# Nine-tap scans with 13 products a line in place of 14, and sums of weights moved to VectorE

## The chip, the cores and the metric

The kernel runs on one core of a Trainium2 chip. The metric is the device time of one execution in microseconds (us); less is better. The engines of the core are TensorE (PE in the profile; PEld is its loading of weights), VectorE (DVE), ScalarE (ACT), GpSimd (POOL) and SyncE (SP), which here only issues transfers. They work at the same time and wait for each other by semaphores. SBUF is the memory on the chip; PSUM holds what TensorE writes.

## The reference

Four layers, each added to its own input after a group normalisation over a float32 image of 2 x 128 channels x 128 x 128: axial attention along one axis, four directional scans, a deformable 3x3 convolution, and a 4x4 convolution with stride 2 in a Hadamard basis. The change is in the second layer, the scans:

```python
def _pass_once(x, w, vertical, reverse):      # w: 128 x 128 x 9
    ...                                       # flipped or transposed for its direction
    def step(carry, xi):
        y = xi + relu(_conv1d(carry, w))      # nine taps along the line, padded by 4
        return (y, y)
    _, ys = lax.scan(step, xs[0], xs[1:])
...
x = _pass_once(x, w_ud, vertical=True, reverse=False)
x = _pass_once(x, w_du, vertical=True, reverse=True)
x = _pass_once(x, w_lr, vertical=False, reverse=False)
x = _pass_once(x, w_rl, vertical=False, reverse=True)
```

Each line of 128 pixels needs the finished line before it, so a scan is 127 dependent steps, and the four scans follow each other.

## The kernel before

Channels lie on the 128 partitions. Both images are held in one tile `both` (views `res[n]`) and are worked on together: a line is 2 images x 128 pixels, split into even and odd pixels of 2 x 64 each. `program` calls, in turn, the attention (`layer0_attention`), `Merge.run` (which also gives the sum of the input and the attention), `layer1` (the scans), `layer2` and `layer3`.

A scan step in `layer1` (line 1103) works from three SBUF tiles of the line before, `lines[turn]`: even pixels e, odd pixels o, and their sum, each with a margin of four. The nine taps are split into four pairs and one single tap, so that the two outputs of a pair of pixels share work: 14 products for 18. TensorE makes three PSUM groups in this order: `pl0` from e (five products with the even taps), `pl1` from o (four products with the odd taps, 65 columns wide, because the even output reads it at one place and the odd output one place further), `pl2` from the sum (the first tap, and four sums of neighbouring taps that are prepared in `ws`). A product is a float32 matmul of 128x128 weights on 2 x 64 or 2 x 65 columns; the profile records it as two matmuls. Then

- ScalarE copies `pl0` to `c0`;
- VectorE adds `pl1` and `c0` to `v`, and a relu-add (`scalar_tensor_tensor`: larger of v and 0, plus the line's own input) writes the new even pixels;
- VectorE adds the shifted `pl1` and `c0` to `u`, subtracts it from `pl2`, and a second relu-add writes the new odd pixels;
- VectorE adds even and odd pixels to the new sum.

In scans 0 to 2 (numbered from 0) ScalarE copies the new pixels back into the image; in scan 3 GpSimd writes them with the layer's input added. In scan 0 ScalarE also normalises each line, four lines ahead (`normalise`). Scans 0 and 1 go over rows, scans 2 and 3 over columns, so that there the image is read and written in strides. PSUM and temporaries have two and three buffers.

The order on TensorE, VectorE, ScalarE and GpSimd within the scans is the order written: they are wrapped in `InOrder` (line 75), which is why nearly everything stands under line 83. Around that, a planner places instructions by when it expects them to be ready: so the first sum of taps, written after the attention, stands on GpSimd's queue among the attention's last instructions, and transfers on SP's queue may pass each other.

`scan_weights` (line 1093) loads a scan's nine taps on ScalarE's queue and has GpSimd add pairs of them to `ws`, in one instruction of 128x512. `prepare()` in `layer1` runs `layer3_weights` (line 1808): it loads the last layer's weights (`ta`) on SP's queue, combines them on GpSimd in 25 operations of 128x256, which fall into the first lines of scan 0, and stores them (`w3_d`). SP's queue also writes the layer's input to `x1_d` and re-sorts it into column blocks, eight copies to `x1c_d` (line 1138), which scan 3 reads.

Of the kernel before, what the change touches and what calls it, by code (L numbers as in the profile page):

```python
# [1091 lines left out]

def scan_weights(env, prm, pool, d):

    nc = env.nc
    wl = pool.tile([P, 9, P], F32, name=f"wl{d}", tag=f"wl{d}")
    nc.scalar.dma_start(out=wl, in_=prm["wscan"][:, d])
    ws = pool.tile([P, 4, P], F32, name=f"ws{d}", tag=f"ws{d}")
    nc.gpsimd.tensor_tensor(ws, wl[:, 2:9:2, :], wl[:, 1:8:2, :], ALU.add)
    return wl, ws  # L1100


def layer1(env, prm, res, both, x1_d, x1c_d, st_gn, st_next, first, prepare):

# [4 lines left out]
    nc, tc = env.nc, env.tc  # L1109
    HS = S // 2  # L1110
    with ExitStack() as ctx:
# [1 line left out]
            for n in range(N):  # L1113
                nc.sync.dma_start(out=x1_d[:, n, lo:hi, :], in_=res[n][:, lo:hi, :])
        cp = ctx.enter_context(tc.tile_pool(name="l1c", bufs=1))
        sp = ctx.enter_context(tc.tile_pool(name="l1s", bufs=3))
        with tc.tile_pool(name="l1pn", bufs=1, space=PSUM) as pn:
            gs, gb = env.group_norm(cp, pn, st_gn, "l1")
        pp = ctx.enter_context(tc.tile_pool(name="l1ps", bufs=2, space=PSUM))
        weights = [first] + [scan_weights(env, prm, cp, d) for d in range(1, 4)]  # L1120
        prepare()
        xp = ctx.enter_context(tc.tile_pool(name="l1x", bufs=2))


        lines = [
            [cp.tile([P, N, HS + 4], F32, name=f"ln{k}{j}", tag=f"ln{k}{j}") for k in range(3)]
            for j in range(2)
        ]
        for pair in lines:
            for t in pair:  # L1130
                nc.vector.memset(t, 0.0)
        pe, dve, act, pool = (
            InOrder(tc, e) for e in (nc.tensor, nc.vector, nc.scalar, nc.gpsimd)
        )
# [16 lines left out]
        def normalise(h):  # L1151
            for n in range(N):
                act.activation(
                    res[n][:, h, :],
                    res[n][:, h, :],
                    AF.Identity,
                    bias=gb[:, n : n + 1],
                    scale=gs[:, n : n + 1],
                )


        ahead = 4
        for h in range(ahead):
            normalise(h)
        turn = 0
        for d in range(4):
            steps = list(range(S)) if d % 2 == 0 else list(range(S - 1, -1, -1))
            wl, ws = weights[d]
            if d == 3:
                columns = {w0: load_columns(w0) for w0 in (S - CB, S - 2 * CB)}  # L1170
            for at, line in enumerate(steps):
                here = [
                    both[:, :, line, k::2] if d < 2 else both[:, :, k::2, line] for k in range(2)
                ]
                if d == 0 and line + ahead < S:
                    normalise(line + ahead)
                last, now = lines[turn], lines[1 - turn]
                turn = 1 - turn
                new = [t[:, :, 2 : 2 + HS] for t in now]
# [5 lines left out]
                if at == 0:  # L1185
                    for k in range(2):
                        dve.tensor_copy(new[k], here[k])
                    dve.tensor_tensor(new[2], new[0], new[1], ALU.add)
                    if d == 3:
                        for k in range(2):  # L1190
                            pool.tensor_tensor(here[k], new[k], add[k], ALU.add)
                    continue
                ps = [
                    pp.tile([P, N, HS + (k == 1)], F32, name=f"pl{k}", tag=f"pl{k}")
                    for k in range(3)
                ]
                for k in range(3):
                    taps = 4 if k == 1 else 5
                    for j in range(taps):
# [10 lines left out]
                            start=(j == 0),  # L1210
                            stop=(j == taps - 1),
                        )
                c0 = sp.tile([P, N, HS], F32, name="c0", tag="c0")
                u = sp.tile([P, N, HS], F32, name="u", tag="u")
                v = sp.tile([P, N, HS], F32, name="v", tag="v")
                act.copy(c0, ps[0])
                dve.tensor_tensor(v, ps[1][:, :, 0:HS], c0, ALU.add)
                dve.scalar_tensor_tensor(new[0], v, 0.0, here[0], ALU.max, ALU.add)
                dve.tensor_tensor(u, ps[1][:, :, 1 : HS + 1], c0, ALU.add)
                v = sp.tile([P, N, HS], F32, name="v", tag="v")  # L1220
                dve.tensor_tensor(v, ps[2], u, ALU.subtract)
                dve.scalar_tensor_tensor(new[1], v, 0.0, here[1], ALU.max, ALU.add)
                dve.tensor_tensor(new[2], new[0], new[1], ALU.add)
                if d == 0:

                    for k in range(2):
                        for n in range(N):
                            act.copy(res[n][:, line, k::2], new[k][:, n])
                    continue
                if d < 3:  # L1230
                    for k in range(2):
                        act.copy(here[k], new[k])
                    continue
                for k in range(2):
                    pool.tensor_tensor(here[k], new[k], add[k], ALU.add)
                if line % RT >= 2 and line < S - RT:
# [559 lines left out]
def layer3_views(t):  # L1796


    a, b = 8 * P, 8 * P + 4 * P
    ws = t[:, 0:a].rearrange("p (k y o) -> p k y o", y=2, o=P)  # L1800
    wt = [
        part.rearrange("p (k r y o) -> p k r y o", r=2, y=2, o=P // 2)
        for part in (t[:, a:b], t[:, b : b + 8 * P])
    ]
    return ws, wt


def layer3_weights(env, prm, w3_d):

    nc, tc = env.nc, env.tc  # L1810
    H = P // 2
    one, two = slice(0, H), slice(H, P)
    add, sub = ALU.add, ALU.subtract
    with tc.tile_pool(name="l3w", bufs=1) as wp:
        ta = wp.tile([P, 4, 4, P], F32, name="ta", tag="ta")
        tb = wp.tile([P, 4, 4, P], F32, name="tb", tag="tb")
        tk = [wp.tile([P, 4, 2, H], F32, name=f"tk{k}", tag=f"tk{k}") for k in range(2)]
        w3 = wp.tile([P, W3], F32, name="w3w", tag="w3w")
        ws, wt = layer3_views(w3)
        nc.sync.dma_start(out=ta.rearrange("p u v o -> p (u v o)"), in_=prm["w3"])  # L1820
        pool = nc.gpsimd
        zero = wp.tile([P, 2 * P], F32, name="zero", tag="zero")
        pool.memset(zero, 0.0)

        def less(to, a, b):

            pool.tensor_tensor(to, a, b, add)
            none = zero.rearrange("p (k o) -> p k o", o=H)
            if len(to.shape) == 4:
                none = zero.rearrange("p (k y o) -> p k y o", y=2, o=H)  # L1830
            pool.tensor_tensor(to, none, to, sub)

        firsts = ((0, 3, add), (0, 3, sub), (2, 1, add), (2, 1, sub))
        seconds = ((3, 1, sub), (3, 1, add), (2, 0, sub), None)
        for part, plan in ((one, firsts), (two, seconds)):
            for k in range(4):
                to = tb[:, k, :, part]
                if plan[k] is None:
                    less(to, ta[:, :, 2, part], ta[:, :, 0, part])
                else:  # L1840
                    x, y, op = plan[k]
                    pool.tensor_tensor(to, ta[:, :, x, part], ta[:, :, y, part], op)
        for half, (part, plan) in enumerate(((one, firsts), (two, seconds))):
            for k in range(4):
                to = ws[:, :, k, part] if k < 2 else tk[half][:, :, k - 2, :]
                if plan[k] is None:
                    less(to, tb[:, :, 2, part], tb[:, :, 0, part])
                else:
                    x, y, op = plan[k]
                    pool.tensor_tensor(to, tb[:, :, x, part], tb[:, :, y, part], op)  # L1850
        for half in range(2):
            x, y = (tk[half][:, k : k + 2] for k in (0, 2))
            to = [wt[half][:, k] for k in range(2 + 2 * half)]
            pool.tensor_tensor(to[0], x, y, add)
            pool.tensor_tensor(to[1], x, y, sub)
            if half == 1:
                pool.tensor_tensor(to[2], y, x, sub)
                less(to[3], x, y)
        nc.sync.dma_start(out=w3_d, in_=w3)


def layer3(env, prm, res, w3_d, st_gn, out):
# [174 lines left out]
def program(ctx, tc, prm, out):  # L2037
# [33 lines left out]
    res = [both[:, n] for n in range(N)]  # L2071
    with tc.tile_pool(name="l1w", bufs=1) as wp:
        first = scan_weights(env, prm, wp, 0)
        merge.run(prm, res, mv, st_gn[1])
        merging.close()
        layer1(
            env,
            prm,
            res,
            both,  # L2080
            x1_d,
            x1c_d,
            st_gn[1],
            st_gn[0],
            first,
            lambda: layer3_weights(env, prm, w3_d),
        )
    layer2(env, prm, res, mem, tables, st_gn[0], st_gn[1])
    layer3(env, prm, res, w3_d, st_gn[1], out)
# [130 lines left out]
```

## Time and profile before

| what | us |
|---|---|
| median of 3 runs (5308.6 to 5312.2) | 5308.91 |
| profiled execution, its own time | 5305.85 |
| its span, first to last instruction | 5304.1 |
| scan 0, from its first sum of a line to that of scan 1 | 405.8 |
| scan 1, the same | 398.6 |
| scan 2, the same | 409.3 |
| scan 3, first to last sum | 417.1 |

TensorE is busy for 4974.9 us of the span, VectorE for 3521.7, ScalarE for 2658.8, GpSimd for 2126.1. The granted TensorE clock is 1.00 in the scans.

How to read it: a row of the timeline has the start in us, the duration in us, the engine, the line of the code, the operation, what it writes and from what, and how many instructions were merged; in brackets stands how long the engine had been idle and what ended that. A row of a tile's answer has the engine, operation, count, shortest/median/longest duration in ns, and the first and last start. `pl` stands for all three PSUM groups, `ln` for all of a line's tiles, `c` for `c0`. A busy TensorE is not TensorE at its peak, and idle time of an engine that nobody waits for costs nothing.

### The profile page before, as it was taken

How to read it: one execution, taken by the hardware profiler on the slowest of the kernel's cores; microseconds unless marked ns; L12 is line 12 of the kernel's file. 1: busy time of each engine (PE TensorE's matmuls, PEld its weight loads, DVE VectorE, ACT ScalarE, POOL GpSimd, SP SyncE). 2: the span in 40 equal slices, each digit the busy share in tenths (PEclk: the TensorE clock that was granted, in tenths of full speed). 3: DMA queues.
4: the chain of work that ended last, by engine and by line, in shares of the span. 5: the costliest groups of instructions: out<-in, count | busy, mean ns of one | idle time of the engine just before them, and what ended most of it. 6: DMA issues, size and time to landing. Idle time of an engine off the chain costs nothing. (4 is left out here: it accounts for less than half of the span.)

```text
span 5304.1 us, 179050 instructions
## 1 busy us (share of the span) xinstructions
PE 4974.9 (94%) x76283; PEld 4306.7 (81%) x76283; DVE 3521.7 (66%) x6818; ACT 2658.8 (50%) x7718; POOL 2126.1 (40%) x1749
## 2 busy tenths in 40 slices
PE   7898999999999934999999999999989999999999
PEld 6767888888888834999999999998468888888777
DVE  3636888888888857555555555666346666666688
ACT  3557898888889845554222332001334443443322
POOL 3214666666666634000000000333035555555576
PEclk8998999999999966999999999999989999999999
DMA  4362333333333369970000000101321111111011
GB/s 160 122 252 63 62 62 61 58 61 62 59 59 63 61 258 305 92 65 2 1 1 1 1 1 1 49 33 38 117 69 35 35 33 38 33 33 32 35 53 57
DMA packets 499988, 347.61 MB, mean 66 GB/s; under 512 B 311669, under 2 KB 456565, under 8 KB 487281
## 3 DMA queue, kind: packets, MB, share of 16 engines
q1 hardware_dynamic: 494144, 326.50, 27.0%
q8 instruction: 607, 9.95, 0.8%
q10 hardware_dynamic: 5040, 9.56, 0.5%
q14 instruction: 197, 1.61, 0.1%
HBM read 194.99 MB, written 157.72 MB: 66 GB/s over the span
## 5 line engine op out<-in xcount | busy, mean ns | idle before, releaser
L83 PE MATMUL pl<-ln,wl 128*128 128x128 f32 (+1 forms) x10160 | 1241.2, 276 | 9.3 <-DVE ln L83 7.8
L83 PEld LDWEIGHTS pl<-ln,wl 128*128 128x128 f32 x10160 | 1176.1, 190 | 22.3 <-issue 6.7
L83 POOL TENSOR_TENSOR w<-d 128x504 f32<-128x504 f32 x512 | 558.6, 1115 | 669.4 <-DVE s L83 612.8
L83 ACT ACTIVATE e<-e,mx 128x128 f32<-128x128 f32 x2048 | 793.4, 395 | 0.8 <-DVE mx L83 0.8
L83 POOL TENSOR_TENSOR res<-ln,x1t 128x128 f32<-128x128 f32 x256 | 149.3, 584 | 1428.2 <-DVE ln L83 1428.2
L83 POOL TENSOR_TENSOR e<-e,total 128x1024 f32<-128x1024 f32 x256 | 485.9, 1898 | 486.4 <-DVE total L83 477.1
L83 ACT COPY res<-ln 128x64 f32<-128x64 f32 (+1 forms) x1016 | 283.9, 304 | 702.2 <-DVE ln L83 702.2
L83 ACT COPY sm<-ps_s 128x1152 f32<-128x1152 f32 x256 | 286.6, 1119 | 562.6 <-PE ps_s L83 562.6
L83 PE MATMUL po<-sm,wdef 128*128 128x256 f32 x2304 | 567.5, 392 | 0.0
L83 PEld LDWEIGHTS ps_s<-s,xw 28*128 28x128 f32 x10240 | 456.6, 187 | 122.2 <-issue 77.2
L83 PE MATMUL pl<-ln,ws 128*128 128x128 f32 x4064 | 536.8, 273 | 0.0
L83 PE MATMUL ps_s<-s,xw 28*128 28x240 f32 (+2 forms) x10240 | 520.0, 343 | 16.4 <-DMA xw<-px_d 13.9
L83 POOL COPY et<-et 128x1024 f32<-128x1024 f32 x256 | 516.4, 2017 | 35.2 <-DVE et L83 27.0
L83 DVE TENSOR_TENSOR v<-pl,c 128x128 f32<-128x128 f32 x508 | 148.1, 291 | 540.7 <-PE pl L83 537.4
L83 PEld LDWEIGHTS pl<-ln,ws 128*128 128x128 f32 x4064 | 494.5, 190 | 0.0
L83 ACT ACTIVATE r<-gen,alphas 128x1536 f32<-128x1536 f32 x256 | 395.0, 1543 | 170.6 <-PE gen L83 143.6
L83 PEld LDWEIGHTS po<-sm,wdef 128*128 128x128 f32 x2304 | 418.4, 190 | 71.0 <-issue 0.2
L83 ACT ACTIVATION_READ_ACCUMULATOR e<-e,mx 128x1 f32 x2048 | 396.5, 194 | 0.0
L83 DVE SCALAR_TENSOR_TENSOR ln<-v,res 128x128 f32<-128x128 f32 x1016 | 347.0, 342 | 48.5 <-POOL res L83 0.9
L83 DVE STREAM_TRANSPOSE s<-w 128x1152 f32<-128x1152 f32 x256 | 349.8, 1367 | 33.0 <-PE ps_s L83 29.9
L83 PE MATMUL te<-cst_main,e 128*128 128x128 f32 x2048 | 338.5, 287 | 28.7 <-POOL e L83 20.9
L83 DVE COPY et<-te 128x512 f32<-128x512 f32 x512 | 348.2, 680 | 12.9 <-PE te L83 12.4
(246 smaller groups left out, 8405.5 us busy)
## 6 DMA issues: line engine op xcount, KB each, us to landing
xw<-px_d SPq DMA_DIRECT2D x528, 56.0 KB
xa<-in_x SPq DMA_DIRECT2D x16, 1024.0 KB
v_d<-vs SPq DMA_DIRECT2D x16, 1024.0 KB
qb_d<-sb SPq DMA_DIRECT2D x16, 1024.0 KB
qa_d<-sa SPq DMA_DIRECT2D x8, 2048.0 KB
zz<-qb_d SPq DMA_DIRECT2D x1024, 16.0 KB
vt<-v_d SPq DMA_DIRECT2D x64, 256.0 KB
qk<-qa_d SPq DMA_DIRECT2D x256, 64.0 KB
```

What stands on the lines that cost most here:

```text
L83: return lambda *a, **k: self.tc.keep_in_program_order(issue(*a, **k))
```

## The change

A step of scans 0 to 2 has five PSUM groups from five inputs: e, o, the sum, and differences that GpSimd now makes. `de` is e one place further less e; `do` is o less o one place further; `t` is e less o. The products are, in TensorE's order: u (three, e with taps 4, 6, 8), d (one, `de` with tap 2), v (two, o with taps 3, 5), b (one, the sum with `ws[4]`), v again (o with tap 7, and `t` with `ws[5]`), q (three from the sum with the sums of taps, one from `do` with tap 0): 13. `ws[4]` and `ws[5]` are half of tap 0 plus tap 2, plus and minus half of tap 1. VectorE has eight operations a line for six, GpSimd four for none. Scan 3 keeps the old step and its 14 products. PSUM has one buffer of each group, temporaries two (v three).

The sums of taps of scan 0 stay on GpSimd (`first_sums`); those of scans 1 to 3 and the weights of layer 3 go to VectorE, one operation after each line of scan 0 from the seventeenth on (`chores`). The load of layer 3's weights is written after the eight column copies. `normalise` of a later line is issued after ScalarE's second copy in place of ahead of the line's first.

```diff
 def scan_weights(env, prm, pool, d):
-    nc.gpsimd.tensor_tensor(ws, wl[:, 2:9:2, :], wl[:, 1:8:2, :], ALU.add)
...
+def first_sums(nc, pool, weights):
+    wl, ws = weights
+    half = pool.tile([P, 1], F32, name="half", tag="half")
+    nc.gpsimd.memset(half, 0.5)
+    nc.gpsimd.tensor_tensor(ws[:, 0:4, :], wl[:, 2:9:2, :], wl[:, 1:8:2, :], ALU.add)
+    nc.gpsimd.tensor_tensor(ws[:, 5, :], wl[:, 0, :], wl[:, 2, :], ALU.add)
+    nc.gpsimd.tensor_tensor(ws[:, 4, :], ws[:, 5, :], wl[:, 1, :], ALU.add)
+    nc.gpsimd.tensor_tensor(ws[:, 5, :], ws[:, 5, :], wl[:, 1, :], ALU.subtract)
+    nc.gpsimd.tensor_tensor(
+        ws[:, 4:6, :], ws[:, 4:6, :], half.unsqueeze(2).to_broadcast([P, 2, P]), ALU.mult
+    )
+
+def sums_of_taps(dve, weights, last):
+    wl, ws = weights
+    for k in (0, 2):
+        dve.tensor_tensor(
+            ws[:, k : k + 2, :],
+            wl[:, 2 * k + 2 : 2 * k + 5 : 2, :],
+            wl[:, 2 * k + 1 : 2 * k + 4 : 2, :],
+            ALU.add,
+        )
+        yield
+    if last:
+        return
+    dve.tensor_tensor(ws[:, 5, :], wl[:, 0, :], wl[:, 2, :], ALU.add)
+    yield
+    dve.tensor_scalar(ws[:, 4, :], ws[:, 5, :], 0.5, None, ALU.mult)
+    yield
+    dve.scalar_tensor_tensor(ws[:, 4, :], wl[:, 1, :], 0.5, ws[:, 4, :], ALU.mult, ALU.add)
+    yield
+    dve.tensor_tensor(ws[:, 5, :], ws[:, 4, :], wl[:, 1, :], ALU.subtract)
+    yield
...
-        sp = ctx.enter_context(tc.tile_pool(name="l1s", bufs=3))
+        sp = ctx.enter_context(tc.tile_pool(name="l1s", bufs=2))
...
-        pp = ctx.enter_context(tc.tile_pool(name="l1ps", bufs=2, space=PSUM))
+        pp = ctx.enter_context(tc.tile_pool(name="l1ps", bufs=1, space=PSUM))
         weights = [first] + [scan_weights(env, prm, cp, d) for d in range(1, 4)]
-        prepare()
-        xp = ctx.enter_context(tc.tile_pool(name="l1x", bufs=2))
...
+        later = layer3_weights(env, prm, w3_d, wp, dve)
+        next(later)
+
+        def chores():
+            for d in range(1, 4):
+                yield from sums_of_taps(dve, weights[d], d == 3)
+            yield from later
+
+        def difference_even(turn):
+            e = lines[turn][0]
+            pool.tensor_tensor(
+                steep[turn][0], e[:, :, 1 : 1 + HS], e[:, :, 0:HS], ALU.subtract
+            )
+
+        def differences_odd(turn):
+            e, o, _, t = lines[turn]
+            inside = slice(2, 2 + HS)
+            pool.tensor_tensor(t[:, :, inside], e[:, :, inside], o[:, :, inside], ALU.subtract)
+            pool.tensor_tensor(
+                steep[turn][1], o[:, :, 0:HS], o[:, :, 1 : 1 + HS], ALU.subtract
+            )
+
+        def products(turn, wl, ws):
+            e, o, both_sum, t = lines[turn]
+            de, do = steep[turn]
+            ps = {
+                k: pp.tile([P, N, HS + (k in "vb")], F32, name=f"p{k}", tag=f"p{k}")
+                for k in "udvbq"
+            }
+            def put(k, w, rhs, start, stop):
+                pe.matmul(ps[k], lhsT=w, rhs=rhs, start=start, stop=stop)
+            for j in (2, 3, 4):
+                put("u", wl[:, 2 * j, :], e[:, :, j : j + HS], j == 2, j == 4)
+            put("d", wl[:, 2, :], de, True, True)
+            for j in (2, 3):
+                put("v", wl[:, 2 * j - 1, :], o[:, :, j - 1 : j + HS], j == 2, False)
+            put("b", ws[:, 4, :], both_sum[:, :, 0 : HS + 1], True, True)
+            put("v", wl[:, 7, :], o[:, :, 3 : HS + 4], False, False)
+            put("v", ws[:, 5, :], t[:, :, 0 : HS + 1], False, True)
+            for j in (2, 3, 4):
+                put("q", ws[:, j - 1, :], both_sum[:, :, j : j + HS], j == 2, False)
+            put("q", wl[:, 0, :], do, False, True)
+            return ps
+
+        def step(d, line, turn, new, here, wl, ws):
+            ps = products(1 - turn, wl, ws)
+            c0, cb = small("c0"), small("cb")
+            act.copy(c0, ps["u"])
+            a = small("a")
+            dve.tensor_tensor(a, ps["d"], c0, ALU.add)
+            act.copy(cb, ps["b"][:, :, 1 : HS + 1])
+            a1 = small("a1")
+            dve.tensor_tensor(a1, ps["b"][:, :, 0:HS], a, ALU.add)
+            b0 = small("b0")
+            pool.tensor_tensor(b0, cb, c0, ALU.subtract)
+            if d == 0 and line + ahead < S:
+                normalise(line + ahead)
+            v = small("v")
+            dve.tensor_tensor(v, ps["v"][:, :, 0:HS], a1, ALU.add)
+            dve.scalar_tensor_tensor(new[0], v, 0.0, here[0], ALU.max, ALU.add)
+            difference_even(turn)
+            b = small("b")
+            dve.tensor_tensor(b, b0, ps["v"][:, :, 1 : HS + 1], ALU.subtract)
+            v = small("v")
+            dve.tensor_tensor(v, ps["q"], b, ALU.add)
+            dve.scalar_tensor_tensor(new[1], v, 0.0, here[1], ALU.max, ALU.add)
+            dve.tensor_tensor(new[2], new[0], new[1], ALU.add)
+            differences_odd(turn)
...
+                if d < 3:
+                    step(d, line, turn, new, here, wl, ws)
+                    if d == 0 and at >= 16:
+                        next(todo, None)
                     continue
...
+def layer3_weights(env, prm, w3_d, wp, dve):
...
+    nc.sync.dma_start(out=ta.rearrange("p u v o -> p (u v o)"), in_=prm["w3"])
+    yield
+    def put(to, x, y, op):
+        if op is None:
+            dve.scalar_tensor_tensor(to, x, -1.0, y, ALU.mult, ALU.subtract)
+        else:
+            dve.tensor_tensor(to, x, y, op)
...
+            put(tb[:, k, :, part], ta[:, :, x, part], ta[:, :, y, part], op)
+            yield
...
+    nc.sync.dma_start(out=w3_d, in_=w3)
...
         first = scan_weights(env, prm, wp, 0)
+        first_sums(nc, wp, first)
         merge.run(prm, res, mv, st_gn[1])
```

More of the change, by code (lines that the diff above doesn't have):

```diff
@@ L1093, in scan_weights, with layer1 @@
 def scan_weights(env, prm, pool, d):
-    nc = env.nc
     wl = pool.tile([P, 9, P], F32, name=f"wl{d}", tag=f"wl{d}")
-    nc.scalar.dma_start(out=wl, in_=prm["wscan"][:, d])
-    ws = pool.tile([P, 4, P], F32, name=f"ws{d}", tag=f"ws{d}")
-    nc.gpsimd.tensor_tensor(ws, wl[:, 2:9:2, :], wl[:, 1:8:2, :], ALU.add)
+    env.nc.scalar.dma_start(out=wl, in_=prm["wscan"][:, d])
+    ws = pool.tile([P, 4 + 2 * (d < 3), P], F32, name=f"ws{d}", tag=f"ws{d}")
     return wl, ws
-def layer1(env, prm, res, both, x1_d, x1c_d, st_gn, st_next, first, prepare):
+def first_sums(nc, pool, weights):
[29 more added lines that the diff above has]
+    yield
+def layer1(env, prm, res, both, x1_d, x1c_d, st_gn, st_next, first, w3_d):
     nc, tc = env.nc, env.tc
@@ L1115, in layer1 @@
         cp = ctx.enter_context(tc.tile_pool(name="l1c", bufs=1))
-        sp = ctx.enter_context(tc.tile_pool(name="l1s", bufs=3))
+        sp = ctx.enter_context(tc.tile_pool(name="l1s", bufs=2))
         with tc.tile_pool(name="l1pn", bufs=1, space=PSUM) as pn:
             gs, gb = env.group_norm(cp, pn, st_gn, "l1")
-        pp = ctx.enter_context(tc.tile_pool(name="l1ps", bufs=2, space=PSUM))
+        pp = ctx.enter_context(tc.tile_pool(name="l1ps", bufs=1, space=PSUM))
         weights = [first] + [scan_weights(env, prm, cp, d) for d in range(1, 4)]
-        prepare()
-        xp = ctx.enter_context(tc.tile_pool(name="l1x", bufs=2))
         lines = [
-            [cp.tile([P, N, HS + 4], F32, name=f"ln{k}{j}", tag=f"ln{k}{j}") for k in range(3)]
+            [cp.tile([P, N, HS + 4], F32, name=f"ln{k}{j}", tag=f"ln{k}{j}") for k in range(4)]
             for j in range(2)
@@ L1131, in layer1 @@
                 nc.vector.memset(t, 0.0)
+        steep = [
+            [cp.tile([P, N, HS], F32, name=f"df{k}{j}", tag=f"df{k}{j}") for k in range(2)]
+            for j in range(2)
+        ]
+        early = ctx.enter_context(ExitStack())
+        wp = early.enter_context(tc.tile_pool(name="l3w", bufs=1))
         pe, dve, act, pool = (
@@ new lines, in small @@
+        def small(name):
+            return sp.tile([P, N, HS], F32, name=name, tag=name, bufs=2 + (name == "v"))
+        def step(d, line, turn, new, here, wl, ws):
[22 more added lines that the diff above has]
+            differences_odd(turn)
+            for k in range(2):
+                if d == 0:
+                    for n in range(N):
+                        act.copy(res[n][:, line, k::2], new[k][:, n])
+                else:
+                    act.copy(here[k], new[k])
@@ L1165, in layer1 @@
         turn = 0
+        todo = chores()
         for d in range(4):
@@ L1170, in layer1 @@
                 columns = {w0: load_columns(w0) for w0 in (S - CB, S - 2 * CB)}
+            elif d == 1:
+                early.close()
+                xp = ctx.enter_context(tc.tile_pool(name="l1x", bufs=2))
             for at, line in enumerate(steps):
@@ L1174, in layer1 @@
                 ]
-                if d == 0 and line + ahead < S:
-                    normalise(line + ahead)
                 last, now = lines[turn], lines[1 - turn]
@@ L1191, in layer1 @@
                             pool.tensor_tensor(here[k], new[k], add[k], ALU.add)
+                    else:
+                        difference_even(turn)
+                        differences_odd(turn)
+                    if d == 0:
+                        normalise(line + ahead)
+                    continue
+                if d < 3:
+                    step(d, line, turn, new, here, wl, ws)
+                    if d == 0 and at >= 16:
+                        next(todo, None)
                     continue
                 ps = [
-                    pp.tile([P, N, HS + (k == 1)], F32, name=f"pl{k}", tag=f"pl{k}")
-                    for k in range(3)
+                    pp.tile([P, N, HS + (k == 1)], F32, name=f"pl{k}", tag=f"p{tag}")
+                    for k, tag in enumerate("uvq")
                 ]
@@ L1212, in layer1 @@
                         )
-                c0 = sp.tile([P, N, HS], F32, name="c0", tag="c0")
-                u = sp.tile([P, N, HS], F32, name="u", tag="u")
-                v = sp.tile([P, N, HS], F32, name="v", tag="v")
+                c0, u = small("c0"), small("a")
+                v = small("v")
                 act.copy(c0, ps[0])
@@ L1219, in layer1 @@
                 dve.tensor_tensor(u, ps[1][:, :, 1 : HS + 1], c0, ALU.add)
-                v = sp.tile([P, N, HS], F32, name="v", tag="v")
+                v = small("v")
                 dve.tensor_tensor(v, ps[2], u, ALU.subtract)
@@ L1223, in layer1 @@
                 dve.tensor_tensor(new[2], new[0], new[1], ALU.add)
[L1224 to L1233, printed above, removed]
                 for k in range(2):
@@ L1805, in layer3_views @@
     return ws, wt
-def layer3_weights(env, prm, w3_d):
-    nc, tc = env.nc, env.tc
+def layer3_weights(env, prm, w3_d, wp, dve):
+    nc = env.nc
     H = P // 2
@@ L1813, in layer3_weights @@
     add, sub = ALU.add, ALU.subtract
[L1814 to L1859, printed above, removed]
@@ new lines, in layer3_weights @@
+    ta = wp.tile([P, 4, 4, P], F32, name="ta", tag="ta")
+    tb = wp.tile([P, 4, 4, P], F32, name="tb", tag="tb")
+    tk = [wp.tile([P, 4, 2, H], F32, name=f"tk{k}", tag=f"tk{k}") for k in range(2)]
+    w3 = wp.tile([P, W3], F32, name="w3w", tag="w3w")
+    ws, wt = layer3_views(w3)
+    nc.sync.dma_start(out=ta.rearrange("p u v o -> p (u v o)"), in_=prm["w3"])
[3 more added lines that the diff above has]
+            dve.scalar_tensor_tensor(to, x, -1.0, y, ALU.mult, ALU.subtract)
+        else:
+            dve.tensor_tensor(to, x, y, op)
@@ new lines, in layer3_weights @@
+    firsts = ((0, 3, add), (0, 3, sub), (2, 1, add), (2, 1, sub))
+    seconds = ((3, 1, sub), (3, 1, add), (2, 0, sub), (2, 0, None))
+    for part, plan in ((one, firsts), (two, seconds)):
+        for k in range(4):
+            x, y, op = plan[k]
+            put(tb[:, k, :, part], ta[:, :, x, part], ta[:, :, y, part], op)
+            yield
+    for half, (part, plan) in enumerate(((one, firsts), (two, seconds))):
+        for k in range(4):
+            to = ws[:, :, k, part] if k < 2 else tk[half][:, :, k - 2, :]
+            x, y, op = plan[k]
+            put(to, tb[:, :, x, part], tb[:, :, y, part], op)
+            yield
@@ L1862, in layer3 @@
+    for half in range(2):
+        x, y = (tk[half][:, k : k + 2] for k in (0, 2))
+        to = [wt[half][:, k] for k in range(2 + 2 * half)]
+        put(to[0], x, y, add)
+        yield
+        put(to[1], x, y, sub)
+        yield
+        if half == 1:
+            put(to[2], y, x, sub)
+            yield
+            put(to[3], x, y, None)
+            yield
+    nc.sync.dma_start(out=w3_d, in_=w3)
 def layer3(env, prm, res, w3_d, st_gn, out):
@@ L2085, in program @@
             first,
-            lambda: layer3_weights(env, prm, w3_d),
+            w3_d,
         )
```

## The prediction

> **What bounds the kernel now.** First the page's busy rows and its 40 slices: TensorE is busy in nearly every slice, and slices 16 to 28 (some 133 us each) are the four scans that the change rewrites.
>
> ```profile
> PE 4974.9 (94%) x76283; PEld 4306.7 (81%) x76283; DVE 3521.7 (66%) x6818; ACT 2658.8 (50%) x7718; POOL 2126.1 (40%) x1749
> ...
> PE   7898999999999934999999999999989999999999
> ```
>
> A share is an average, so next the pace of each scan, from the one sum per line (`ln<-ln,ln`), asked for in a stretch of scan 1, 2 and 3 in turn (scans count from 0):
>
> ```profile
> L83 DVE TENSOR_TENSOR ln<-ln,ln x123: 292/293/295, 2475.5 to 2857.0; 128x128 f32<-128x128 f32 x123
> ...
> L83 DVE TENSOR_TENSOR ln<-ln,ln x123: 292/293/296, 2877.4 to 3269.0; 128x128 f32<-128x128 f32 x123
> ...
> L83 DVE TENSOR_TENSOR ln<-ln,ln x107: 292/293/296, 3299.8 to 3647.4; 128x128 f32<-128x128 f32 x107
> ```
>
> Last start minus first, over one less than the count: 3.127, 3.210 and 3.279 us a line. The number of products is the same, so TensorE's work alone does not set all three. The timeline of scan 1, then of scan 2, shows what does:
>
> ```profile
> 2602.86 2.40 PE L83 MATMUL pl<-ln,wl 128*128 128x128 f32 x20
> 2603.05 0.29 DVE L83 TENSOR_TENSOR v<-pl,u 128x128 f32<-128x128 f32 x1 [0.23 <-PE pl L83]
> ...
> 2605.09 1.06 PE L83 MATMUL pl<-ln,ws 128*128 128x128 f32 x8
> 2605.14 0.29 DVE L83 TENSOR_TENSOR v<-pl,c 128x128 f32<-128x128 f32 x1 [1.14 <-PE pl L83]
> ...
> 3001.11 0.38 DVE L83 SCALAR_TENSOR_TENSOR ln<-v,res 128x128 f32<-128x128 f32 x1
> ...
> 3001.63 1.91 PE L83 MATMUL pl<-ln,wl 128*128 128x128 f32 x15
> ```
>
> A product is two records. 28 records a line at 0.1117 us apart fill 3.127: scans 0 and 1 are bound by the products. Beside that runs a **chain**: the even pixels of a line must exist before the next line's first product. Records one by one give it: first product to `v<-pl,c`, nine products later, 2.36 us (when the first product had to wait, as in scan 2); v 0.29; a gap 0.03; the relu-add (SCALAR_TENSOR_TENSOR) 0.29; its end to the next first product 0.15. That is 3.12, just hidden under 3.127. In scan 2 the relu-add reads columns and takes 0.38: 3.21, the measured pace. In scan 3 it takes 0.38 and its gap is 0.10, for a second semaphore: 3.28, again as measured. So the model has been tested three times, and **removing a product from a line gains only what the chain gives up**.
>
> **The change, part by part.** *The chain.* In the new order (u three, d, v two, b, v two, then q four) the product that completes v is again the ninth. What changes is the wait: in the rows above `v<-pl,c` starts 0.27 after the product following its group (2605.09 less two records), `v<-pl,u` only 0.20 (2603.05 against 2602.86). The records show why: the first waits for TensorE in a separate semaphore instruction and then for ScalarE; the second for VectorE in the separate one and for TensorE itself. The new v reads PSUM and a1, which VectorE writes: the second pair. Chain: 2.36 - 0.07 + 0.29 + 0.03 + 0.29 + 0.15 = 3.05 in scans 0 and 1, 3.14 in scan 2; the thirteen products, 26 records, take 2.90 and are covered. Gain 0.077 x 127 = 9.8 in each of scans 0 and 1, 0.07 x 127 = 8.9 in scan 2. Scan 3 keeps its form; its single PSUM buffers are read long before they are rewritten (c0 by ScalarE, the rest before the odd pixels that gate the same products), so 0. **28.5 us gained.** If v kept the old wait, all of it would be gone.
>
> *What has to fit beside it*, from a line's first product at 0. b is complete at the seventh product; a1 can start at 1.84 and ends at 2.13, before v at 2.29 (cover 0.13). ScalarE's copy cb runs 1.89 to 2.16. GpSimd's b0 is a form the trace lacks; its nearest rows are
>
> ```profile
> L552 POOL TENSOR_TENSOR acc<-acc,prod x32: 462/466/472, 245.8 to 388.1; 128x132 f32<-128x132 f32 x32
> L83 POOL TENSOR_TENSOR res<-ln,x1t x214: 525/586/649, 3299.9 to 3649.5; 128x128 f32<-128x128 f32 x107
> ```
>
> the first contiguous, the second strided: I take 0.46, bounds 0.46 and 0.58. With 0.08 to 0.15 to start, b0 ends at 2.70 to 2.77. The relu-add starts at 2.61. VectorE's b waits for b0; behind it in VectorE's order stand the second v, the odd relu-add and the sum, and TensorE waits for the odd pixels: b may start at 2.82 anyway (order), so nothing is late. The odd pixels come at 3.80 + 0.12 against a weight load due at 3.91: no cover left, but it costs only its own lateness. The even difference starts after the relu-add (2.90) plus 0.15 for two semaphores, ends at 3.51, and d's weights are due at 3.68 (cover 0.1). The two odd differences end near 4.9, that is 1.9 into the next line, before b0 at 2.25. GpSimd carries 4 x 0.46 of 3.05. ScalarE in scan 0 carries c0, cb, the moved normalise (0.88) and four copies, 2.2 of 3.05; the copies behind normalise delay the next c0 by at most 0.2, under the 0.25 that a has.
>
> *The port between GpSimd and VectorE.* In scan 0 of before, GpSimd built layer 3's weights:
>
> ```profile
> 2106.53 0.29 DVE L83 TENSOR_TENSOR v<-pl,u 128x128 f32<-128x128 f32 x1
> 2106.78 0.72 POOL L1827 TENSOR_TENSOR tb<-ta 128x256 f32<-128x256 f32 x1
> 2106.86 0.79 DVE L83 SCALAR_TENSOR_TENSOR ln<-v,res 128x128 f32<-128x128 f32 x1
> ```
>
> The relu-add, two SBUF inputs, ends 0.15 after GpSimd's (2107.50): its last 0.14 waited. The PSUM form kept 0.29. The Trainium skill ("SBUF — State Buffer", SBUF: two separate sides) states the rule that speaks against this change: the shared pair is an exclusive lock for the whole instruction, and the loser blocks fully. If each relu-add lost to a whole GpSimd operation, a line would be 3.05 + 0.46 = 3.51, 146 us worse over 381 lines. By the row only an overlap with the relu-add's last 0.14 counts: for the even one, 2.76 to 2.90, against b0's end at 2.70 to 2.77. I go by the row and allow 0.01 a line: **3.8 us lost**.
>
> *Layer 3's weights and the sums of taps.* GpSimd's 26 operations leave scan 0: its five stretched lines (one 0.98, four 0.45 over) return, **2.8 gained**. 36 VectorE operations come in, one after each line from the seventeenth on. 128x256 is between 0.29 (128 wide) and 1.23 (128x1024): some 0.43, into the idle stretch between the sum (1.07 in the next line) and a (1.30). Alone it is covered by a1's wait; held by a GpSimd difference it ends at 1.65 and v is 0.04 late: **1.5 lost**, bounds 0 and 11. The load of these weights now stands behind the eight column copies on SP's queue, the store behind VectorE's last part, near 2225; copies held behind that store are wanted only by scan 3 (3280). For the load see the rivals. *first_sums* puts some four more GpSimd operations (three 0.46, one 0.75) where one stands now:
>
> ```profile
> 1905.20 1.26 POOL L1099 TENSOR_TENSOR ws<-wl 128x512 f32<-128x512 f32 x1 [4.43 <-DMA wl<-in_wscan]
> ...
> 1908.37 0.71 PEld L83 LDWEIGHTS te<-cst_main,e 128*128 128x128 f32 x4 [5.16 <-POOL e L83]
> ```
>
> TensorE waits there for e, so **2.1 lost**; bounds -5 (the sums fall behind e) and 2.1. Two more memsets ahead of the scans **0.3 lost**; line 1 no longer has its two normalises (0.88) ahead of c0, **0.9 gained**. SBUF buffers cut from three to two: all readers are a line old, 0.
>
> Sum: -28.5 + 3.8 - 2.8 + 1.5 + 2.1 + 0.3 - 0.9 = -24.5. The profiled run took 5305.85 (span 5304.1), so 5281.4; the median shown is 3.06 above it: **5284**.
>
> **Rivals.** *Products bind* (the diff's plain promise): 0.223 x 381 = 85, 5224. It needs a chain under 2.90, and scan 2's pace speaks against it. *v keeps the 0.27 wait*: the gain 28.5 goes, 5309 to 5313. *GpSimd too slow, the other sign*: place, b0 before the even relu-add. At 0.58 an operation (the mean of the strided form) b0 ends at 2.85, the relu-add at 2.99, and the even difference makes d late by 0.05: 3.19 a line, 0.06 over before, +23: 5332. It decides from b0 ending at 2.84; for it speaks the strided row, against it the contiguous one. *The load stays behind the copies*: of the eight copies one was issued at 2098.61 and seven over 157 us to 2281; a load behind all lands near 2292, while VectorE, in order, wants it at line 31, near 2160: all stops for some 132 us, 5416. It decides from more than two copies ahead. Against it: before, a copy passed a store that was not ready, and the copies wait for their rows' stores (2098.61) while the load waits for nothing.
>
> **Chances and range.** 0.2% (10.6 us) is about what a measurement of this kernel tells from no change. Forecast 0.58 (alone 5272 to 5298: sums behind e and no losses below, the losses doubled above), v's wait 0.10, products 0.04, GpSimd 0.19, load 0.09. Faster 0.58 + 0.04 + 0.02 of v's case = 0.64; same 0.08; slower 0.19 + 0.09 = 0.28. From 5268 to 5336: out stay the products, the load and a quarter of the GpSimd case.
>
> **What would show it.** Paces of 3.05, 3.05, 3.14, 3.28; TensorE idle before the first product of a line, for the even pixels; `a1`, `b0` ended before v and the relu-add's last part; relu-adds still 0.29 and 0.38; no DMA wait on VectorE in scan 0. Wrong: a relu-add over 0.35, GpSimd operations over 0.55, TensorE waiting for d, or v 0.27 behind its product.

## The result and the profile after

The changed kernel takes **5389.58 us** (5383.8 to 5394.4), the kernel before, beside it, 5308.76: ratio **1.0154, interval 1.0141 to 1.0167**. It is 81 us slower where 25 us faster was forecast. The profiled execution took 5389.32 us (span 5387.5, 83.4 over before).

The page's busy row and its slices, of the kernel after:

```profile
PE 4987.4 (93%) x75521; PEld 4257.1 (79%) x75521; DVE 3754.7 (70%) x7618; ACT 2727.0 (51%) x8099; POOL 2770.0 (51%) x3258
...
PE   7888999999999916999999999999989999999999
```

TensorE has 762 records fewer (76283 to 75521, the 381 products) and is still busy in tenths of 9 all through the scans: a record is counted for 0.27 us though the next can follow 0.11 behind it, so that of a line's 3.33 only 0.16 counts as idle, and the slices hide the loss. The paces don't. The one sum per line, asked for in a stretch of scans 1, 2 and 3:

```profile
L83 DVE TENSOR_TENSOR ln<-ln,ln x121: 293/294/295, 2500.8 to 2899.9; 128x128 f32<-128x128 f32 x121
...
L83 DVE TENSOR_TENSOR ln<-ln,ln x123: 292/293/296, 2925.2 to 3352.1; 128x128 f32<-128x128 f32 x123
...
L83 DVE TENSOR_TENSOR ln<-ln,ln x110: 292/293/524, 3362.6 to 3719.8; 128x128 f32<-128x128 f32 x110
```

By last start less first, over one less than the count, scan 1 goes at 3.326 and scan 2 at 3.499 us a line (before: 3.127 and 3.210). Scan 3 keeps its 3.28. By stage, from the sums' starts in both profiled executions:

| stage | forecast | measured |
|---|---|---|
| start of scan 0 (first sum) | +2.4 | +2.1 |
| scan 0 | -10.7 | +19.9 |
| scan 1 | -8.5 | +25.4 |
| scan 2 | -7.6 | +36.8 |
| scan 3 | 0 | +1.0 |
| after the scans | 0 | -1.8 |
| sum | -24.5 | +83.4 |

So the loss lies wholly in the scans with the new step. One line of scan 1 in the timeline after (start, duration, engine, operation, in brackets how long the engine sat idle and what ended that):

```profile
2599.77 0.91 PE L83 MATMUL pu<-ln,wl 128*128 128x128 f32 x6 [0.16 <-DVE ln L83]
...
2600.40 0.30 PEld L83 LDWEIGHTS pd<-df,wl 128*128 128x128 f32 x2
...
2600.66 0.52 PEld L83 LDWEIGHTS pv<-ln,wl 128*128 128x128 f32 x4
...
2601.21 0.39 PE L83 MATMUL pb<-ln,ws 128*128 128x130 f32 x2
...
2601.64 0.27 ACT L83 COPY cb<-pb 128x128 f32<-128x128 f32 x1 [0.59 <-PE pb L83]
2601.66 0.38 PE L83 MATMUL pv<-ln,ws 128*128 128x130 f32 x2
...
2601.88 0.83 PE L83 MATMUL pq<-ln,ws 128*128 128x128 f32 x6
2601.93 0.29 DVE L83 TENSOR_TENSOR a<-pb,a 128x128 f32<-128x128 f32 x1 [0.57 <-ACT cb L83]
2602.05 0.46 POOL L83 TENSOR_TENSOR b<-cb,c 128x128 f32<-128x128 f32 x1 [0.49 <-ACT cb L83]
2602.33 0.29 DVE L83 TENSOR_TENSOR v<-pv,a 128x128 f32<-128x128 f32 x1
...
2602.66 0.29 DVE L83 SCALAR_TENSOR_TENSOR ln<-v,res 128x128 f32<-128x128 f32 x1
...
2603.10 0.57 PE L83 MATMUL pu<-ln,wl 128*128 128x128 f32 x3 [0.16 <-DVE ln L83]
```

From first product to first product: 3.33. `a<-pb,a` is a1. It reads PSUM group b, done since about 2601.6, and a; and it starts at 2601.93, released by **ScalarE's copy cb**, whose result it doesn't read. The copy reads the same group b, is written ahead of a1, and a1 waits for its end. v, which should start 0.20 behind the product following its group (2601.88), starts 0.45 behind: 0.25 late. That this happens in every line is seen when the tile a is asked for, scan 1 of after (first column us, second times):

```profile
its engine sat idle before it (us, times) until:
  ACT cb L83: 50.6, 90
  ACT c L83: 18.5, 90
```

All 90 waits of a1 in that stretch end with cb. The trace also keeps, for each instruction, the numbers of the semaphores that it waits for. In all 381 lines a1 waits for ScalarE's, which cb counts up, and for VectorE's own, and not for TensorE's, though TensorE writes its input. So the turn stands in the program, as a semaphore; that PSUM itself would hold up a second reader is shown by no run here.

### The profile page after: what moved, and what is told of

Read it like the earlier page. It is cut to its first block, busy times and chain, and to the rows that moved or that the text cites. A ratio compares the mean times of both kernels' runs of the same rounds, so it can differ in the third digit from the quotient of the medians.

```text
span 5387.5 us, 182503 instructions
## 1 busy us (share of the span) xinstructions
PE 4987.4 (93%) x75521; PEld 4257.1 (79%) x75521; DVE 3754.7 (70%) x7618; ACT 2727.0 (51%) x8099; POOL 2770.0 (51%) x3258
## 5 line engine op out<-in xcount | busy, mean ns | idle before, releaser
L83 POOL TENSOR_TENSOR df<-ln 128x128 f32<-128x128 f32 x768 | 310.1, 404 | 244.3 <-DVE ln L83 241.0
L83 PE MATMUL pu<-ln,wl 128*128 128x128 f32 x2286 | 345.9, 286 | 76.7 <-DVE ln L83 76.5
L83 PE MATMUL pv<-ln,wl 128*128 128x130 f32 x2286 | 396.2, 281 | 0.0
L83 PEld LDWEIGHTS pu<-ln,wl 128*128 128x128 f32 x2286 | 284.1, 189 | 138.1 <-issue 134.2
L83 PE MATMUL gen<-zz,toep 32*128 32x128 f32 x8192 | 334.3, 289 | 22.0 <-DMA zz<-qb_d 14.6
L83 PEld LDWEIGHTS gen<-zz,toep 32*128 32x128 f32 x8192 | 283.1, 190 | 77.8 <-issue 65.5
```

Of the source, the lines that this page charges most:

```text
L83: return lambda *a, **k: self.tc.keep_in_program_order(issue(*a, **k))
```

## The experiments

The theory: two engines that read one PSUM group take turns in the order in which their reads are written, and the copy ahead of a1 costs 0.25 a line. Rivals: the single PSUM buffers; the port between GpSimd and VectorE; VectorE's added operations, by their number or by the length of the chain a, a1, v; something outside the step. The names e1 to e12 are those that the expectations use.

**e1, the order of the two reads.**

```diff
-            act.copy(cb, ps["b"][:, :, 1 : HS + 1])
             a1 = small("a1")
             dve.tensor_tensor(a1, ps["b"][:, :, 0:HS], a, ALU.add)
+            act.copy(cb, ps["b"][:, :, 1 : HS + 1])
```

> VectorE's a1 written ahead of ScalarE's copy cb; the same instructions, the two reads of the PSUM group b in the other order. Theory (two engines' reads of one PSUM group are put in the order written, so a1 waits for cb): a1 starts some 0.3 us earlier, right behind b's product, and v no longer waits for a1; but cb now waits for a1, so b0 on GpSimd runs to about 3.05 us after the line's first product, into the even relu-add's last part, which should then take some 0.5 instead of 0.29: a pace of 3.3 again, 5370 to 5395. If the port does not hold the relu-add: 3.05 a line, about 5285. Rival (single PSUM buffers, or VectorE simply has too many operations): nothing moves, 3.32 and 5389, with a relu-add of 0.29.

Measured: 5412.2, ratio 1.0194 (1.0177 to 1.0211), paces of scans 0, 1 and 2: 3.350, 3.347, 3.523. Timeline of a line of scan 1:

```profile
2600.99 0.29 DVE L83 TENSOR_TENSOR a<-pb,a 128x128 f32<-128x128 f32 x1 [0.27 <-PE pb L83]
...
2601.24 0.83 PE L83 MATMUL pq<-ln,ws 128*128 128x128 f32 x6
2601.32 0.27 ACT L83 COPY cb<-pb 128x128 f32<-128x128 f32 x1 [0.92 <-DVE a L83]
2601.44 0.29 DVE L83 TENSOR_TENSOR v<-pv,a 128x128 f32<-128x128 f32 x1 [0.15 <-PE pv L83]
2601.73 0.46 POOL L83 TENSOR_TENSOR b<-cb,c 128x128 f32<-128x128 f32 x1 [0.82 <-ACT cb L83]
2601.77 0.56 DVE L83 SCALAR_TENSOR_TENSOR ln<-v,res 128x128 f32<-128x128 f32 x1
...
2602.48 0.91 PE L83 MATMUL pu<-ln,wl 128*128 128x128 f32 x6 [0.18 <-DVE ln L83]
```

The turn is reversed: a1 is now released by TensorE, and the copy waits for a1; in all 381 lines the semaphore that a1 waits for is now TensorE's, and the copy's is VectorE's. v is on time (0.20 behind the following product), but b0 on GpSimd, now 0.32 later in the line, runs over the even relu-add, which takes 0.56 in place of 0.29 and ends 0.14 after GpSimd does (2602.19). The 0.25 won ahead of v are lost behind it: the edit shows the wait, and cannot show its price.

**e2, b0 on VectorE, no copy.**

```diff
-            act.copy(cb, ps["b"][:, :, 1 : HS + 1])
-            pool.tensor_tensor(b0, cb, c0, ALU.subtract)
+            dve.tensor_tensor(b0, ps["b"][:, :, 1 : HS + 1], c0, ALU.subtract)
```

> No copy cb and no b0 on GpSimd: VectorE takes b0 from PSUM itself, between a1 and v, so that one engine alone reads the group b. Theory (a1's wait for cb): paces of 3.05, 3.05 and 3.14 to 3.20, so 0.27 x 254 + 0.32 x 127 = 110 us less than the changed kernel: about 5280. Rival (VectorE has too much to do: nine operations a line for eight): the pace stays at 3.3 or rises, 5389 or more. Rival (single PSUM buffers): 5389.

Measured: 5361.85, ratio 1.0101 (1.0083 to 1.0118), paces 3.218, 3.217, 3.397. Better than after by 28, but far from what was expected. A line of scan 1:

```profile
2601.11 0.29 DVE L83 TENSOR_TENSOR a<-pb,a 128x128 f32<-128x128 f32 x1 [0.27 <-PE pb L83]
...
2601.35 0.83 PE L83 MATMUL pq<-ln,ws 128*128 128x128 f32 x6
2601.55 0.29 DVE L83 TENSOR_TENSOR v<-pv,a 128x128 f32<-128x128 f32 x1
...
2601.95 0.29 DVE L83 SCALAR_TENSOR_TENSOR ln<-v,res 128x128 f32<-128x128 f32 x1
```

v is on time, but the relu-add starts 0.11 after v's end where it was 0.03. It overwrites a line that GpSimd's differences have read, so VectorE must wait until GpSimd has read it; in the changed kernel b, which reads b0 from GpSimd, had met that wait. With b0 on VectorE no other instruction did, and the wait moved to both relu-adds, on the chain: the trace has GpSimd's semaphore on them here, and on b there.

**e3, two PSUM buffers for the groups v, b and q.**

```diff
-                k: pp.tile([P, N, HS + (k in "vb")], F32, name=f"p{k}", tag=f"p{k}")
+                k: pp.tile([P, N, HS + (k in "vb")], F32, name=f"p{k}", tag=f"p{k}", bufs=1 + (k in "vbq"))
```

> The PSUM groups v, b and q get two buffers each[...], nothing else. Theory (a1's wait for cb): no change, 5389. Rival (TensorE or the readers wait for single buffers): the pace falls toward 3.05, 5285 to 5310.

Measured: 5412.95, ratio 1.0194 (1.0177 to 1.0211), paces 3.379, 3.380, 3.553. The single buffers aren't the cause. That double ones cost 0.055 a line was not expected; cb starts 0.37 behind the start of b's last record in place of 0.31, which is all of it (medians of scan 1), and it has come to wait for a second semaphore beside TensorE's.

**e4, all but the step.** The old step in scans 0 to 2, everything else as after (`if d < 3: step(...)` taken out, its old branches put back).

> The old step with 14 products in all scans, with everything else of the change: sums of taps and layer 3's weights on VectorE, first_sums, single PSUM buffers. Theory (the loss is in the new step): paces of 3.127, 3.127 and 3.21 as before, and the rest costs what was forecast, -2.8 + 1.5 + 2.1 + 0.3: 5308 to 5313. Rival (VectorE's 36 operations stretch their lines by 0.3 each): some 5320. Rival (single PSUM buffers cost): a pace over 3.2 in scans 0 and 1, over 5330.

Measured: 5305.55, ratio 0.9992 (0.9984 to 1.0001), paces 3.127, 3.126, 3.210, 3.280: those of before. The sums of weights on VectorE, the load behind the column copies and the buffers cost nothing that can be told. (The normalise stands at its old place here.) The loss is in the step.

For the sums and weights on VectorE that holds with the old step alone. The first combinations of layer 3's weights, after and here:

```profile
L83 DVE TENSOR_TENSOR tb<-ta x7: 682/684/684, 2170.2 to 2190.2; 128x256 f32<-128x256 f32 x7
...
L83 DVE TENSOR_TENSOR tb<-ta x7: 417/418/420, 2168.4 to 2187.2; 128x256 f32<-128x256 f32 x7
```

Beside GpSimd's differences one takes 0.68, without them 0.42. In the changed kernel a1's wait for cb hides that; in the kernels without the copy that follow, the 36 lines with such an operation are 2.3 to 3.1 us longer in all than as many later ones.

**e5, the copy alone.** This kernel leaves out b's share of the odd pixels.

```diff
-            act.copy(cb, ps["b"][:, :, 1 : HS + 1])
...
-            pool.tensor_tensor(b0, cb, c0, ALU.subtract)
+            pool.tensor_tensor(b0, c0, c0, ALU.add)
```

> The changed kernel without ScalarE's copy cb; GpSimd's b0 adds c0 to itself instead, at the same place, so that VectorE alone reads the group b and still meets GpSimd once a line. This leaves out the sum of weights' share of the odd pixels. Theory (a1's wait for cb is the loss): a1 starts right behind its product, v behind its own, paces of 3.05 to 3.10 in scans 0 and 1 and 3.14 to 3.25 in scan 2, so some 5285 to 5300. Rival (the length of the VectorE chain a, a1, v, whatever cb does): 3.25 or more, over 5360.

Measured: 5298.81, ratio 0.9989 (0.9982 to 0.9996), paces 3.078, 3.077, 3.258. A line of scan 1:

```profile
2600.36 0.29 DVE L83 TENSOR_TENSOR a<-pb,a 128x128 f32<-128x128 f32 x1 [0.27 <-PE pb L83]
...
2600.60 0.83 PE L83 MATMUL pq<-ln,ws 128*128 128x128 f32 x6
...
2600.80 0.29 DVE L83 TENSOR_TENSOR v<-pv,a 128x128 f32<-128x128 f32 x1 [0.16 <-PE pv L83]
2601.13 0.29 DVE L83 SCALAR_TENSOR_TENSOR ln<-v,res 128x128 f32<-128x128 f32 x1
```

The tile a asked for in this kernel, scan 1, has as its first row in place of cb's:

```profile
  PE pb L83: 24.6, 91
```

With GpSimd doing as many operations as after, and only the copy gone, a1 waits for TensorE, v starts 0.20 behind the following product and each line gives back 0.25, 0.25 and 0.24 in scans 0, 1 and 2. Times 127 that is 94 us, more than the 83.4 lost: **the loss is the copy's turn on group b**.

**e6, the wait for GpSimd moved off the chain.** To the kernel with b0 on VectorE (e2) one instruction is added, a copy of one element that GpSimd wrote, behind the sum:

```diff
             dve.tensor_tensor(new[2], new[0], new[1], ALU.add)
+            dve.tensor_copy(seen, steep[1 - turn][1][:, 0, 0:1])
```

> VectorE takes b0 itself, as in the second experiment, and after each line's sum it copies one element of the last line's odd difference, so that it meets GpSimd's semaphore there and not ahead of the two relu-adds. Theory (in the second experiment the relu-adds had come to need a semaphore instruction of their own, 0.07 each, and the odd one also pushed the next line's odd products): the gap from v to the relu-add is 0.03 again and the paces fall from 3.22, 3.22, 3.40 to 3.07 to 3.12 and 3.17 to 3.28: 5290 to 5315. Rival (ninth and tenth operation fill VectorE): no less than 3.22, 5362.

Measured: 5300.45, ratio 0.9989 (0.9981 to 0.9996), paces 3.076, 3.075, 3.257. A line of scan 1:

```profile
2600.79 0.15 DVE L83 COPY seen<-df 128x1 f32<-128x1 f32 x1
...
2601.89 0.83 PE L83 MATMUL pq<-ln,ws 128*128 128x128 f32 x6
2602.09 0.29 DVE L83 TENSOR_TENSOR v<-pv,a 128x128 f32<-128x128 f32 x1
...
2602.41 0.29 DVE L83 SCALAR_TENSOR_TENSOR ln<-v,res 128x128 f32<-128x128 f32 x1
...
2602.85 0.91 PE L83 MATMUL pu<-ln,wl 128*128 128x128 f32 x6
```

The gap ahead of the relu-add is 0.03 again, and 0.14 a line is won by an instruction that computes nothing: it takes the wait in VectorE's idle time. This kernel computes the whole step with 13 products and ten VectorE operations a line against eight in the changed one, and with the same chain a, a1, v. So neither the number of VectorE's operations nor that chain held the changed kernel at 3.33. At 0.9989 of the kernel before it is hardly faster than that one.

**e7 and e8, the attention's tail.** The forecast's 2.1 us for GpSimd's first sums, timeline after:

```profile
1906.49 1.26 POOL L1106 TENSOR_TENSOR ws<-wl 128x512 f32<-128x512 f32 x1 [4.43 <-DMA wl<-in_wscan]
...
1907.70 0.45 POOL L1107 TENSOR_TENSOR ws<-wl 128x128 f32<-128x128 f32 x1
...
1909.30 0.61 POOL L1110 TENSOR_TENSOR ws<-ws,half 128x256 f32<-128x256 f32 x1
1909.88 1.90 POOL L83 TENSOR_TENSOR e<-e,total 128x1024 f32<-128x1024 f32 x1
...
1911.82 0.29 PEld L83 LDWEIGHTS te<-cst_main,e 128*128 128x128 f32 x2 [7.72 <-POOL e L83]
```

In two kernels the load of the first taps is made to wait for a late statistic (`tensor_copy(wl[:, 0, 0:1], after)` ahead of it), so that the sums fall where GpSimd is idle: one with the old step (e7: e4 with the late load), one with all the remedies (e8: e6 with the late load).

> The old step with the moved sums (the fourth experiment), and the load of scan 0's taps held until the attention's last statistics, by a copy of one element into its tile. Theory (the sums of taps stood on GpSimd's queue ahead of the attention's last operation e and TensorE waited 7.7 us for it): the wait falls to some 2 or 3, so 5 us less than the fourth experiment's 5305.6: 5300. Rival (that wait is hidden or comes back in the merge): 5305.

> The kernel of e6 with the late load of e7. Theory: e6 less 5 us, 5285 to 5310, under the kernel before. Rival: no difference from e6.

Measured: 5301.75, ratio 0.9992 (0.9985 to 0.9998), and 5299.28, ratio 0.9989 (0.9981 to 0.9997): the ratios of the kernels without the late load. In the profile with all the remedies the sums move as meant:

```profile
1921.59 1.27 POOL L1108 TENSOR_TENSOR ws<-wl 128x512 f32<-128x512 f32 x1 [15.00 <-DMA wl<-in_wscan]
```

and scan 0 starts 3.0 earlier than in the kernel without (2062.3 against 2065.3). But that start scatters as much among profiles of kernels that are alike up to it, and the whole runs don't show a gain beyond their scatter. What the wait on e costs at the end stays open.

**e9 to e12, scan 2.** Without the copy it goes at 3.257 where 3.14 was forecast. Timeline of the kernel with the moved wait (e6), scan 2:

```profile
2988.55 0.38 DVE L83 SCALAR_TENSOR_TENSOR ln<-v,res 128x128 f32<-128x128 f32 x1
2988.70 0.30 PEld L83 LDWEIGHTS pd<-df,wl 128*128 128x128 f32 x2
...
2989.05 0.52 PEld L83 LDWEIGHTS pv<-ln,wl 128*128 128x128 f32 x4
```

The odd pixels' relu-add ends at 2988.93, and the weights of v, which read the odd pixels, start 0.12 later: 0.35 after the weights of d, where two records take 0.22. So a line of scan 2 pays for both relu-adds of 0.38: for the even one ahead of its first product, and for the odd one in 0.12 that TensorE waits ahead of v. Four kernels follow from that. The first three (e9, e10, e11) are the one with all the remedies (e8) and one edit more, the fourth (e12) is the kernel before with e11's copies alone. The first edit puts the old step back in scan 2:

```diff
-                if d < 3:
+                if d < 2:
                     step(d, line, turn, new, here, wl, ws)
```

> The kernel of e8 with the old step of 14 products in scan 2; scans 0 and 1 keep the new step with b0 on VectorE. Theory (scan 2's reading of columns makes the relu-adds 0.38, and with the old step only the even one counts): paces 3.08, 3.08, 3.21, 3.28; scan 2 gains 0.047 x 127 = 6 against e8, so some 5293, ratio about 0.998. Rival (scan 2's 3.26 comes from the strided image and not from the step): 3.26 again, the time of e8.

The second has ScalarE copy the next line's columns in scan 2 (VectorE's b then shares its buffers with a, to make room); in the third and fourth the same stands in scan 3 too, which runs backwards, so that the next line is the one at line - 1:

```diff
+        def fetch(line):
+            if 0 <= line < S:
+                ahead_cols[line] = [small(f"h{k}") for k in range(2)]
+                for k in range(2):
+                    act.copy(ahead_cols[line][k], both[:, :, k::2, line])
...
             act.copy(c0, ps["u"])
+            if d == 2:
+                fetch(line + 1)
...
-            dve.scalar_tensor_tensor(new[0], v, 0.0, here[0], ALU.max, ALU.add)
+            dve.scalar_tensor_tensor(new[0], v, 0.0, own[0], ALU.max, ALU.add)
```

> The kernel of e8; in scan 2 ScalarE copies the next line's even and odd columns into two contiguous tiles right after its copy c0, and the relu-adds read those. Theory (the relu-adds' 0.38 on strided columns is all that sets scan 2 apart from scan 1): relu-adds 0.29, pace 3.08 in scan 2 as in scans 0 and 1, 0.18 x 127 = 23 less than e8, some 5276, ratio 0.995. Rival (ScalarE's added 0.8 us a line makes the next c0 or the copies into the image late): 3.2 or more, 5290 to 5300.

> e10, and the same copies ahead in scan 3, whose step stays the old one. Theory: scan 3's chain gives up 0.09 for the even relu-add, 3.28 to 3.19, 11 less than e10: some 5265, ratio 0.993. Rival (scan 3 is held by GpSimd's two strided additions or its semaphore, not by the length of the relu-add): 3.28 stays, the time of e10.

> The kernel before with nothing but the copies ahead in scans 2 and 3. Theory: scan 2's chain 3.21 less 0.09 is 3.12, so its 14 products bind at 3.127 (10.5 gained); scan 3 goes from 3.28 to 3.19 (11.4 gained): some 5283 to 5287, ratio 0.996, and what e11 has beyond that, some 18, is what the new step is worth once its copy is gone. Rival (scan 3 held by GpSimd): only 10.5, ratio 0.998.

| kernel | us | ratio, interval | paces of scans 1, 2, 3 |
|---|---|---|---|
| e9, old step in scan 2 | 5292.59 | 0.9971 (0.9960 to 0.9983) | 3.08, 3.21, 3.28 |
| e10, columns ahead in scan 2 | 5279.64 | 0.9947 (0.9933 to 0.9961) | 3.08, 3.08, 3.28 |
| e11, columns ahead in scans 2 and 3 | 5270.64 | 0.9929 (0.9916 to 0.9943) | 3.08, 3.08, 3.19 |
| e12, before, columns ahead in 2 and 3 | 5286.23 | 0.9960 (0.9947 to 0.9974) | 3.13, 3.13, 3.19 |

The kernel before took 5309.88 beside these. All the paces came as the theory had them. The group of relu-adds of scan 3 in the third of them:

```profile
L83 DVE SCALAR_TENSOR_TENSOR ln<-v,h x214: 292/293/298, 3300.0 to 3638.6; 128x128 f32<-128x128 f32 x107
```

293 ns from contiguous tiles where before took 0.38 from columns. The third kernel is **39 us faster than before**; 24 of that the old step gets too (the fourth), and 16 are what the third has beyond it. The step of 13 products accounts for some 18 in scans 0 to 2, (3.127 - 3.08) x 381; its chain, not its products, then sets the 3.08. The two kernels also differ in the moved sums and loads.

## Why the prediction was wrong

**The step that failed** is "b is complete at the seventh product; a1 can start at 1.84 and ends at 2.13, before v at 2.29 (cover 0.13)". It took a1's start from its inputs alone. Beside it the text placed ScalarE's copy cb, 1.89 to 2.16, on the same group, and put the order of the two reads at nothing. From a line's first product, cb in fact ran 1.87 to 2.13, a1 waited for its end and ran 2.16 to 2.46, and v, due at 2.29, started at 2.56. The kernel without the copy has a1 at its place (1.87) and the loss gone; that is shown. Whether two engines could read one group at once if nothing ordered them wasn't tried.

**The rest of the working, point by point.**

- *The chain as the bound, and products that gain only what the chain gives up*: right. Without the copy the paces are 3.08, against 14 products' 3.127 and the 2.90 that 13 products fill by the forecast's estimate. "Products bind" fell.
- *v's wait, 0.07 less*: right wherever a1 is in time (0.20 behind the following product, in e1, e2, e5 and e6). The rival "v keeps the 0.27 wait" fell. 3.05 was forecast; the missing 0.03 is the odd pixels' "own lateness", which the text named and put at nothing: the weights of v, which read the odd pixels, start 0.26 after those of d in place of 0.22 (2600.66 and 2600.40 in scan 1 after).
- *3.14 in scan 2*: mis-sized. It put 0.09 for the even relu-add and left out the 0.09 of the odd one, for which TensorE waits as well: 3.257 measured without the copy, 0.12 x 127 = 15 us.
- *GpSimd's b0, 0.46*: measured 0.46. "GpSimd too slow" fell: TensorE did not wait for its differences; the weights of d load 0.11 behind u's last ones, in scans 1 and 2.
- *The port*: in the kernel after both relu-adds stayed at 0.29 in scan 1, so the 3.8 allowed weren't lost. The swapped order (e1) has the case that was feared, and it comes out by the row that the forecast went by, not by a whole GpSimd operation: 0.56, ended 0.14 after GpSimd. By the Trainium skill ("SBUF — State Buffer", SBUF: two separate sides) the loser blocks for the whole of the other's instruction; here the relu-add, started 0.04 behind GpSimd's operation, lost 0.27 to its 0.46: it was held past GpSimd's end, but not by a whole operation. VectorE's operations with an input in PSUM, run under GpSimd's, kept their 0.29.
- *Layer 3's weights, 36 operations on VectorE, the load behind the copies*: the weights were there in time, and "the load stays behind the copies" fell. The 1.5 for operations held by a GpSimd difference is right in kind: nothing in e4, which has no differences, hidden behind a1's wait in the changed kernel, 2.3 to 3.1 once the copy is gone. (GpSimd's operations on the weights were 25 in the trace before, not 26.)
- *first_sums, 2.1*: TensorE's wait for e rose from 5.16 to 7.72, and scan 0 starts 2.1 later in the profile after. That the two figures agree is luck: in the profiles of the seven kernels with the same first sums (the changed one, e1 to e6) this start lies anywhere from 2064.4 to 2071.1.
- *Scan 3 unchanged*: +1.0.

In the sum, the forecast -24.5, the copy's turn 94, the odd pixels 0.03 x 254 + 0.12 x 127 = 23, less the port's 3.8 that weren't spent, make 89; 83.4 were measured in the profiled spans. Scans 1 and 2 come out to 0.1; 3.4 of the 5 between lie in scan 0. Two things there were not in the sum: the 1.5 that stayed hidden, and that before two lines in every sixteen are 0.35 longer together, 2.4 in all, which are gone after; why, stays open.

## What to carry to other kernels

When an instruction is placed by when its inputs are ready, also list who else reads the same PSUM group ahead of it in program order: the second reader may wait for the first one's end, as it did here in all 381 lines. A wait that leaves one instruction reappears on the next that needs the same news from that engine; a one-element read in idle time can hold it off the chain. And before taking work from an engine that a chain keeps waiting, shorten the chain: relu-adds that read contiguous copies, made by an idle engine a line ahead, gave more here (24 us) than the product taken away (some 16).

## What was not expected of the hardware

- A second reader of a PSUM group on another engine waited, by a semaphore of the program, for the first in both orders: VectorE's a1 started 2.16 behind the line's first product after ScalarE's copy and 1.87 without it; ScalarE's copy 2.19 after a1 and 1.87 ahead of it.
- One more engine to wait for cost VectorE 0.07 ahead of a dependent instruction (0.03 to 0.10, medians of scan 1), and nothing when an idle instruction of 0.15 had waited already.
- Double PSUM buffers of groups v, b and q were slower than single ones by 0.055 a line.
